# Deformable sampling with 9 x 14 source tiles on 126 partitions instead of 8 x 16 on 128

## The chip, the cores and the metric

The kernel runs on one core of a Trainium2 chip. The metric is the device time of one execution in microseconds (us), given as the median of several runs. One profiled execution supplies the trace from which all durations, waits and transfer rates below are read.

## The reference, cut to what matters

Two layers run on an input of 2 images x 256 channels x 128 x 128 pixels. The first has three branches with dilations 1, 9 and 12. Each branch computes 18 offsets per pixel with a 3x3 convolution, samples the normalised image at nine displaced positions with bilinear weights, and sums the nine samples with one weight per channel and tap.

```python
def _deform_dw(x, offset, w, pad, dil):
    ...
    py = yy[None, None] - pad + ky[None, :, None, None] * dil + off[:, :, 0]
    px = xx[None, None] - pad + kx[None, :, None, None] * dil + off[:, :, 1]
    sampled = _bilinear(x, py, px)
    wk = w.reshape(C, K)
    return jnp.einsum('bckhw,ck->bchw', sampled, wk)
def _branch(x, w_off, w_def, lw, lb, pad, dil):
    off = _conv(x, w_off, pad, dil)
    y = _deform_dw(x, off, w_def, pad, dil)
    return jax.nn.gelu(_ln2d(y, lw, lb), approximate=False)
x1 = _branch(x, off_w1, def_w1, bw1, bb1, 1, 1)
x2 = _branch(x, off_w2, def_w2, bw2, bb2, 9, 9)
x3 = _branch(x, off_w3, def_w3, bw3, bb3, 12, 12)
c = jnp.einsum('bchw,oc->bohw', x, conv_w[:, :, 0, 0]) + conv_b[None, :, None, None]
out = _ln2d(x1 + x2 + x3 + c, n1_w, n1_b)
h = out.transpose(0, 2, 3, 1)
h = jax.nn.gelu(h @ mlp_w1.T + mlp_b1, approximate=False) @ mlp_w2.T + mlp_b2
...
x = x + _L0_conv_ref(_gn(x), ...)
x = x + _L1_conv_ref(_gn(x), ...)      # a 3x3 convolution with ternary weights
```

## The kernel before, in words

The kernel has three stages. In the trace they lie at 0 to about 950 us, 958 to about 6460 us, and from there to the end.

**The first stage** (`phase_a`, once per image, with the group norm's statistics ahead of it) walks over the image four rows at a time. It loads four rows of x (`xa`, issued by ScalarE), normalises them, writes them with pixels in rows and channels in columns to a table in DRAM (`table`, padded with zeros on all sides), and multiplies by the offset weights (`pz`, kept in `zr`). Every eight rows `offsets` adds the shifted parts. `make_hats` (four rows per call) turns each offset into "hats": for each tap, and for each of TR row and TC column distances inside a source tile, the value min(|distance|, 1) - 1. The product of a row hat and a column hat is the bilinear weight of one source pixel. The hats of one four-row group are built on NH = TR + TC rows for each of nine (branch, row tap) pairs, four pairs in one tile `hb` and five in the next, and stored in DRAM as `hats[q, hat, y, kx, x]` (line 432, issued by SP, three `hb` buffers). The DMA's outermost dimension is pairs times hats: 4 x 24 = 96 and 5 x 24 = 120 partitions.

**The second stage** (`sample_near`) does the sampling by matmul. A unit is (image, row step Rt, branch). A source tile is TR x TC pixels of the table by 256 channels, one pixel per partition (line 770): 8 x 16 = 128 pixels serve RI x CI = 2 x 10 output positions with a reach of 3 pixels each way. A row step has NT = 14 tiles, shared by its three branches. For each of the up to three row taps ky of a unit, `load_hats` fetches a row hat `hy` and a column hat `hx`, both for all 128 pixels, two rows, three column taps and 128 columns (line 796; one row hat is read again for all TC pixels, one column hat for all TR). `build` multiplies them into the weight tile `A` (line 816, VectorE; two `A` alternate between units). In `sample`, for each channel half c, each tile is a matmul of 128 pixels x 128 channels by A's 9 taps x 2 rows x 10 columns = 180 (line 889); an f32 matmul appears as two instructions. Two tiles share a PSUM tile `pm` (four of them), which ScalarE copies to `ev` (line 898, three buffers). `accumulate` then adds the nine taps, each times its channel weight, into a ring of image rows for the branch: the first by ScalarE (line 860), the other eight by VectorE (line 867). When a ring has four finished rows, a chain of the class `Tail` is started: layer norm, gelu, the sum of the branches in DRAM (`g12d`), and for the last branch the 1x1 convolution, norm and MLP (lines 573 to 745). The tail's steps are interleaved with the sampling by `tail.advance()`, called at fixed points of `sample`, and ahead of need when a ring row is still to be read.

The order of all compute instructions of this stage is fixed by `pin` (program order on each engine). The loads are on SP's queue, which runs in order. `prepare(u + 2)` is called after the second half's matmuls of unit u: it builds all products of unit u + 2 one after the other and then issues the hat loads of unit u + 3, whose buffers (three `hy`, three `hx`) come free with these products. The source tiles have 20 buffers for 14 in use.

**The third stage** (`phase_c_signs`) is the ternary convolution. It is not touched.

The constants that the change sets anew are these:

```python
RI, CI = 2, 10
TR, TC = RI + 2 * REACH, CI + 2 * REACH
NT = -(-(W + 2 * REACH) // CI)
NH = TR + TC
RINGS = (8, 24, 32)
```

Of the kernel before, what the change touches and what calls it, by code (L numbers as in the profile page):

```python
# [9 lines left out]
F32 = mybir.dt.float32  # L10
I32 = mybir.dt.int32
U32 = mybir.dt.uint32
BF16 = mybir.dt.bfloat16
# [28 lines left out]
RI, CI = 2, 10  # L42
# [3 lines left out]
AO = 12  # L46
WA = 28 + W
NH = TR + TC
HALF = 64
RINGS = (8, 24, 32)  # L50
# [6 lines left out]
XCLS = (0, 1, 2, 8, 9)  # L57
# [10 lines left out]
def conv_preact_kernel(ctx: ExitStack, tc: tile.TileContext, t: dict, out: bass.AP):  # L68
# [5 lines left out]
    NR = (H + 2 * REACH) // RI  # L74
# [202 lines left out]
    def phase_a(b, pool, psum, k, beside):  # L277
# [123 lines left out]
        def make_hats(g, parts, r0):  # L401
# [7 lines left out]
            pl = k["planes"][g % 2]  # L409
# [40 lines left out]
    with ExitStack() as actx:  # L450
        psum = actx.enter_context(tc.tile_pool(name="ps_a", bufs=1, space=PSUM))

        def gps():
# [12 lines left out]
            "planes": [ap.tile([P, 2, NG], BF16, name=f"planes{i}") for i in range(2)],  # L466
# [6 lines left out]
        for b in range(NB):  # L473
# [12 lines left out]
            if b == 0:  # L486
# [6 lines left out]
                pattern = ap.tile([P, NG], F32, name="pattern", tag="xt", bufs=3)  # L493
                nc.sync.dma_start(pattern[HALF : HALF + NPAT], t["pattern"])
                for pl in k["planes"]:
                    nc.vector.tensor_copy(
                        pl[HALF : HALF + NPAT, 1, :], pattern[HALF : HALF + NPAT]
                    )
# [23 lines left out]
    def free(ins):  # L522
        return ins

    class Tail:
# [50 lines left out]
        def normalised(self, z, src, what=None):  # L576
# [10 lines left out]
            for h in range(NB4 // 2):  # L587
                tp = self.bank("tp")
                for j in range(2):
                    for c in range(KC):  # L590
                        i = j * KC + c
                        px = slice((2 * h + j) * P, (2 * h + j + 1) * P)
                        pin(nc.tensor.transpose(tp[:, i * P : (i + 1) * P], src[:, c, px], ident))  # L593
# [78 lines left out]
        def finish(self, b, g, S, other, xn):  # L672
# [16 lines left out]
            yield from self.normalised(z, S)  # L689
# [42 lines left out]
            yield from self.normalised(z, S)  # L732
# [19 lines left out]
    def sample_near(pool, psum, k):  # L752
# [7 lines left out]
        def load_tiles(b, Rt):  # L760

            xts[b, Rt] = []
            for T in range(NT):
                xt = pool.tile([P, C], F32, name="xs", tag="xs", bufs=20)
# [5 lines left out]
                nc.sync.dma_start(xt, src)  # L770
# [11 lines left out]
        def load_hats(u):  # L782
            b, Rt, br = units[u]
            for ky in taps(u):
                i0, i1 = valid(Rt, br, ky)
                hq = hats[b][br * 3 + ky + 1]
                y0 = Rt * RI - REACH - ky * DILS[br] + i0
                hy = pool.tile([P, RI, 3, W], F32, name="hy", tag="hy", bufs=3)
                hx = pool.tile([P, RI, 3, W], F32, name="hx", tag="hx", bufs=3)
                pitch = HY * 3 * W  # L790
                for h, first, dims in (
                    (hy, 0, [[0, TC], [pitch, TR]]),
                    (hx, TR, [[pitch, TC], [0, TR]]),
                ):
                    src = hq[first, y0]
                    nc.sync.dma_start(
                        h[:, i0:i1].rearrange("p i t w -> p (i t w)"),
# [520 lines left out]
```

## Time and profile before

| what | value |
|---|---|
| median of three runs | 7621.91 us (7618.33 to 7638.79) |
| the profiled execution | 7634.92 us, its span 7633.1 us |
| mean granted TensorE clock | 0.97 |
| sampling matmuls, line 889 | 22,288 instructions, 318 ns each as recorded |
| hat loads, line 796 | 2 x 1130 |
| source tile loads, line 770 | 1876 of 128 KB |
| hat stores, line 432 | 64 of 720 KB, 64 of 576 KB |

The execution from which the profile was taken is 13 us above the median. Its time is 1.8 us more than the span, which runs from the first to the last instruction. The recorded duration of a matmul includes the time in which it overlaps its neighbours: a burst of 28 sampling matmuls takes 4.43 us, 158 ns each. Windows of the trace list, for each stretch, its length, the busy time and number of instructions of TensorE, of its weight loads, of VectorE, ScalarE and GpSimd, the granted clock, the mean busy share of the 16 DMA engines, and the GB/s they moved. A DMA share a little above 1 means that packets of one engine overlap.

### The profile page before, as it was taken

Reading aid. Unit: us, or ns where it says so; the run is one execution under the profiler, and the core shown is the slowest. Engines: PE = TensorE matmul, PEld = TensorE weight load, DVE = VectorE, ACT = ScalarE, POOL = GpSimd, SP = SyncE. Lnnn points to the kernel's source line nnn. Section 1 sums busy time; section 2 is a strip of 40 time slices with the busy share of each in tenths; the row PEclk is TensorE's granted clock in tenths of the full one; section 3 lists DMA queues with packets and bytes.
Section 4 is the critical chain, followed back from the end, with each engine's and each line's share of the span. In section 5 each row is a group of like instructions: output and inputs, shape, how many; then the busy total and the mean of one; then the engine's idle time right before and its main releaser. Section 6 shows DMA issues by size and latency. Waiting matters only on the chain. (4 is left out here: it accounts for less than half of the span.)

```text
span 7633.1 us, 114421 instructions
## 1 busy us (share of the span) xinstructions
PE 7040.9 (92%) x37984; PEld 5353.3 (70%) x37984; DVE 6109.5 (80%) x12723; ACT 4832.0 (63%) x10150; POOL 712.8 (9%) x1292
## 2 busy tenths in 40 slices
PE   6899888999999999999988999999999999899999
PEld 3555487777887788887777877887888777444444
DVE  7756557888888888988578888888888986677675
ACT  2344366777777777777676777777777777433232
POOL 0000000111111111111100111111111111000000
PEclk9999989999999999999999999999999999899999
DMA  8866689999999999998699999999999995222121
GB/s 285 265 193 197 181 231 250 248 253 256 256 255 252 254 259 255 258 256 231 180 239 246 254 255 253 256 254 253 251 259 254 254 252 161 90 75 76 69 78 47
DMA packets 856311, 1658.87 MB, mean 217 GB/s; under 512 B 116704, under 2 KB 403216, under 8 KB 851480
## 3 DMA queue, kind: packets, MB, share of 16 engines
q1 hardware_dynamic: 838296, 1617.84, 78.1%
q10 hardware_dynamic: 17408, 33.56, 1.3%
q8 instruction: 304, 4.98, 0.3%
q14 instruction: 303, 2.48, 0.1%
HBM read 1381.02 MB, written 270.06 MB: 216 GB/s over the span
## 5 line engine op out<-in xcount | busy, mean ns | idle before, releaser
L889 PE MATMUL pm<-A,xs 128*128 128x180 f32 (+2 forms) x22288 | 3624.6, 318 | 355.6 <-ACT ev L898 248.8
L889 PEld LDWEIGHTS pm<-A,xs 128*128 128x128 f32 x22288 | 3400.5, 195 | 598.0 <-ACT ev L898 347.0
L867 DVE SCALAR_TENSOR_TENSOR ring<-ev,defw,ring 128x256 f32<-128x256 f32 (+3 forms) x6344 | 2780.4, 459 | 339.1 <-ACT ev L898 159.0
L898 ACT COPY ev<-pm 128x360 f32<-128x360 f32 (+2 forms) x5572 | 2244.9, 449 | 791.3 <-PE pm L889 483.3
L816 DVE TENSOR_TENSOR A<-hy,hx 128x768 f32<-128x768 f32 x1130 | 1026.1, 947 | 413.1 <-DMA hx<-hats 300.6
L1172 PE MATMUL pc<-cring,signs 128*128 128x512 bf16 x4608 | 1005.3, 381 | 20.0 <-ACT cring L1119 13.3
L1172 PEld LDWEIGHTS <-signs 128*128 128x128 bf16 x4608 | 452.0, 98 | 572.8 <-issue 27.0
L614 ACT ACTIVATE T<-T,rs 128x256 f32<-128x256 f32 x1280 | 661.9, 589 | 180.5 <-POOL rs L610 180.4
L607 POOL TENSOR_SCALAR rs<-mv 128x4 f32<-128x4 f32 x320 | 122.8, 384 | 4904.3 <-DVE mv L605 2681.5
L573 PE MATMUL hp<-T,w 128*128 128x512 f32 x1024 | 503.8, 617 | 12.9 <-ACT T L692 12.9
L603 DVE BATCH_NORM_STATS2 st<-T 128x6 f32<-128x256 f32 x1280 | 447.0, 412 | 25.3 <-ACT T L595 25.2
L320 PE MATMUL pz<-wz,xa 128*128 128x486 f32 x1024 | 463.7, 582 | 3.1 <-DVE zr L327 3.1
L573 PE MATMUL h<-hT,w 128*128 128x512 f32 x1024 | 460.1, 592 | 0.0
L642 ACT ACTIVATE T<-zc,bb,bw 128x512 f32<-128x512 f32 x384 | 277.5, 773 | 228.0 <-PE zc L626 227.9
L860 ACT ACTIVATE ring<-ev,defw 128x256 f32<-128x256 f32 (+1 forms) x788 | 392.2, 503 | 24.1
L1180 ACT ACTIVATE o<-xl,l1b 128x1024 f32<-128x1024 f32 x64 | 73.5, 1148 | 501.8 <-DMA out_x<-o 394.8
L626 PEld LDWEIGHTS zc<-ident,T 128*128 128x128 f32 x2560 | 315.0, 147 | 96.3 <-issue 61.9
L626 PE MATMUL zc<-ident,T 128*128 128x128 f32 x2560 | 358.7, 284 | 19.7 <-ACT T L614 13.8
L595 ACT COPY T<-tp 128x512 f32<-128x512 f32 x640 | 340.5, 583 | 42.5 <-PE tp L593 42.3
L609 POOL TENSOR_TENSOR rs<-rs,mhalf 128x4 f32<-128x4 f32 x320 | 365.0, 1141 | 0.0
L1119 ACT CAST cring<-D 128x2048 bf16<-128x2048 f32 (+1 forms) x140 | 245.0, 1755 | 183.4 <-PE pc L1172 125.1
L573 PEld LDWEIGHTS h<-hT,w 128*128 128x128 f32 x1024 | 189.1, 190 | 186.6 <-issue 186.1
(118 smaller groups left out, 5226.4 us busy)
## 6 DMA issues: line engine op xcount, KB each, us to landing
hy<-hats SPq DMA_DIRECT2D x1114, 384.0 KB
hx<-hats SPq DMA_DIRECT2D x1114, 384.0 KB
xs<-table SPq DMA_DIRECT2D x1876, 128.0 KB
g12d<-T SPq DMA_DIRECT2D x128, 512.0 KB
other<-g12d SPq DMA_DIRECT2D x128, 512.0 KB
hats<-hb SPq DMA_DIRECT2D x64, 720.0 KB
hats<-hb SPq DMA_DIRECT2D x64, 576.0 KB
xl<-x1d SPq DMA_DIRECT2D x56, 640.0 KB
```

The lines of the kernel that those rows point to most:

```text
L320: nc.tensor.matmul(pz[:, 0:NZ], lhsT=xt[:, c, r, :], rhs=k["wz"][:, c, :], start=c == 0, stop=c == KC - 1,)
L573: nc.tensor.matmul(out, lhsT=w, rhs=v, start=i == 0, stop=i == n - 1)
L603: pin(nc.vector.bn_stats(st[:, j, :], Tv[:, j, :]))
L609: nc.gpsimd.tensor_tensor(rs[:, 0, :], rs[:, 0, :], mhalf[:, 0:NB4], ALU.pow)
L614: nc.scalar.activation(Tv[:, j, :], Tv[:, j, :], AF.Identity, scale=rs[:, 0, j : j + 1], bias=rs[:, 1, j : j + 1],)
L626: nc.tensor.transpose(zc[:, j * P : (j + 1) * P], Tv[:, j, c * P : (c + 1) * P], ident)
L816: nc.vector.tensor_tensor(dst, hy[:, i0:i1].rearrange("p i t w -> p t i w"), hx[:, i0:i1].rearrange("p i t w -> p t i w"), ALU.mult,)
L860: pin(nc.scalar.mul(dst, src, w))
L867: pin(nc.vector.scalar_tensor_tensor(dst, src, w, dst, ALU.mult, ALU.add))
L889: nc.tensor.matmul(pm[:, j, 0:n], lhsT=xts[b, Rt][T + j][:, c * P : (c + 1) * P], rhs=A[:, m0:m1, AO + (T + j) * CI : AO + (T + j + 1) * C ...
L898: nc.scalar.copy(ev[:, m0:m1, T * CI : (T + 2) * CI].rearrange("p m (t j) -> p t m j", j=CI), pm[:, :, 0:n].rearrange("p t (m j) -> p t m ...
L1172: nc.tensor.matmul(pc[:, bank, :], lhsT=w[:, m * P : (m + 1) * P], rhs=xc[:, i, k, t * JC : (t + 1) * JC, kx : kx + W], start=j == 0, stop ...
```

## The change

The source tile becomes 9 x 14 = 126 pixels for 3 x 8 positions: RI, CI = 3, 8. There are then 17 tiles in a row step and 45 row steps instead of 67. NH becomes 9 + 14 = 23. The matmuls have up to 9 x 3 x 8 = 216 columns. The tiles, hats and products are addressed on 126 partitions (TP).

The weight tile `A` is laid out with WP = 136 columns a row and no gap between rows; columns of one tap that no sum reads may hold values of the neighbouring row. `columns` gives, for each tile, which column taps are read at all; others are left out of the matmul and of the copy. The first tile has a PSUM tile of its own, the other sixteen go in pairs.

The products of a unit are no longer built together: `steps` lists all of them in order, and `build(until)` does the next one, if it belongs to a unit not later than `until`. It is called after the matmuls of each half and, in the first half, also in the middle of the sums. Hats are loaded one transfer at a time (`load_hat`), up to two products ahead, into four buffers with one tag. The rings have 9, 25 and 31 rows, and are read row by row by the tail (`by_row`, `rows`), since a group of four may wrap. `ev` has two buffers, the source tiles 23. The tail is advanced three times in each half instead of twice. Where the row pattern of the hats has a period of 3, three `planes` with their own patterns are used in turn. The scratch space reserved for dynamic DMAs is set to 4096 bytes.

```diff
@@ -39,22 +39,29 @@
 
 REACH = 3
 LIMIT = float(REACH)
-RI, CI = 2, 10
+RI, CI = 3, 8
 TR, TC = RI + 2 * REACH, CI + 2 * REACH
 NT = -(-(W + 2 * REACH) // CI)
 WT = NT * CI + 2 * REACH
-AO = 12
-WA = 28 + W
+TP = TR * TC
+WP = NT * CI
+AO = 16
+KA = 9 * WP + AO
+WA = AO + 3 * KA
 NH = TR + TC
 HALF = 64
-RINGS = (8, 24, 32)
+RINGS = (9, 25, 31)
 BRS = (0, 1, 2)
 NORMS = 3
 VBUFS = 9
 PEAK = 3
 GAP = 2
 LAG = 5
-XCLS = (0, 1, 2, 8, 9)
+XBUFS = NT + 6
+HBUFS = 4
+EBUFS = 2
+TICKS = (5, 11)
+XCLS = (0, 1, 4, 7)
 NPAT = RI + len(XCLS) + 1
 
 
...
-    NR = (H + 2 * REACH) // RI
+    NR = -(-(H + 2 * REACH) // RI)
...
-            pl = k["planes"][g % 2]
+            pl = k["planes"][g % RI]
...
-                xt = pool.tile([P, C], F32, name="xs", tag="xs", bufs=20)
+                xt = pool.tile([P, C], F32, name="xs", tag="xs", bufs=XBUFS)
                 src = bass.AP(
                     table[b].tensor,
                     table[b].offset + (Rt * RI * WT + T * CI) * C,
                     [[C, TC], [WT * C, TR], [1, C]],
                 )
-                nc.sync.dma_start(xt, src)
+                nc.sync.dma_start(xt[0:TP], src)
...
-        def load_hats(u):
+        def columns(br, T):
+
+            dil = DILS[br]
+            t = [
+                i
+                for i, s in enumerate((-dil, 0, dil))
+                if max(0, REACH + s) < (T + 1) * CI
+                and T * CI < min(W + 2 * REACH, W + REACH + s)
+            ]
+            return t[0] * RI, (t[-1] + 1) * RI
+
+        steps = [(u, ky) for u in range(len(units)) for ky in taps(u)]
+        loads = [(u, ky, x) for u, ky in steps for x in range(2)]
+        at = {"load": 0, "build": 0}
+
+        def load_hat(u, ky, x):
+
             b, Rt, br = units[u]
-            for ky in taps(u):
-                i0, i1 = valid(Rt, br, ky)
-                hq = hats[b][br * 3 + ky + 1]
-                y0 = Rt * RI - REACH - ky * DILS[br] + i0
-                hy = pool.tile([P, RI, 3, W], F32, name="hy", tag="hy", bufs=3)
-                hx = pool.tile([P, RI, 3, W], F32, name="hx", tag="hx", bufs=3)
-                pitch = HY * 3 * W
-                for h, first, dims in (
-                    (hy, 0, [[0, TC], [pitch, TR]]),
-                    (hx, TR, [[pitch, TC], [0, TR]]),
-                ):
-                    src = hq[first, y0]
-                    nc.sync.dma_start(
-                        h[:, i0:i1].rearrange("p i t w -> p (i t w)"),
-                        bass.AP(src.tensor, src.offset, dims + [[1, (i1 - i0) * 3 * W]]),
-                    )
-                hbs[u, ky] = hy, hx
-
-        def build(u, ky):
-
+            i0, i1 = valid(Rt, br, ky)
+            hq = hats[b][br * 3 + ky + 1]
+            pitch = HY * 3 * W
+            dims = [[pitch, TC], [0, TR]] if x else [[0, TC], [pitch, TR]]
+            src = hq[x * TR, Rt * RI - REACH - ky * DILS[br] + i0]
+            h = pool.tile([P, RI, 3, W], F32, name="h", tag="h", bufs=HBUFS)
+            nc.sync.dma_start(
+                h[0:TP, i0:i1].rearrange("p i t w -> p (i t w)"),
+                bass.AP(src.tensor, src.offset, dims + [[1, (i1 - i0) * 3 * W]]),
+            )
+            hbs[u, ky, x] = h
+
+        def load_hats():
+
+            while at["load"] < min(len(loads), 2 * at["build"] + HBUFS):
+                load_hat(*loads[at["load"]])
+                at["load"] += 1
+
+        def build(until):
+
+            if at["build"] == len(steps) or steps[at["build"]][0] > until:
+                return False
+            u, ky = steps[at["build"]]
             b, Rt, br = units[u]
             dil = DILS[br]
             i0, i1 = valid(Rt, br, ky)
-            hy, hx = hbs.pop((u, ky))
-
...
+            A = k["A"][u % len(k["A"])]
             dst = bass.AP(
-                Af.tensor,
-                Af.offset + ((ky + 1) * 3 * RI + i0) * WA + AO + REACH - dil,
-                [list(Af.ap[0]), [RI * WA + dil, 3], [WA, i1 - i0], [1, W]],
+                A.tensor,
+                A.offset + AO + (ky + 1) * KA + i0 * WP + REACH - dil,
+                [[A.ap[0][0], TP], [RI * WP + dil, 3], [WP, i1 - i0], [1, W]],
             )
             pin(
                 nc.vector.tensor_tensor(
                     dst,
-                    hy[:, i0:i1].rearrange("p i t w -> p t i w"),
-                    hx[:, i0:i1].rearrange("p i t w -> p t i w"),
+                    hy[0:TP, i0:i1].rearrange("p i t w -> p t i w"),
+                    hx[0:TP, i0:i1].rearrange("p i t w -> p t i w"),
                     ALU.mult,
                 )
             )
+            at["build"] += 1
+            load_hats()
+            return True
 
...
-            for ky in reversed(kys):
-                for dst, src, w in sums[ky]:
-                    pin(nc.vector.scalar_tensor_tensor(dst, src, w, dst, ALU.mult, ALU.add))
+            todo = [s for ky in reversed(kys) for s in sums[ky]]
+            for n, (dst, src, w) in enumerate(todo):
+                if c == 0 and n == len(todo) // 2:
+                    build(u + 1)
+                pin(nc.vector.scalar_tensor_tensor(dst, src, w, dst, ALU.mult, ALU.add))
 
         def sample(u, c):
 
             b, Rt, br = units[u]
             kys = taps(u)
+            if c == 0:
+                while build(u):
+                    pass
             tail.advance()
             if not kys:
                 tail.advance()
-                if c == KC - 1:
-                    prepare(u + 2)
+                tail.advance()
+                build(u + 1 + c)
                 return
-            A = k["A"][u % len(k["A"])].rearrange("p t i w -> p (t i) w")
-            m0, m1 = (kys[0] + 1) * 3 * RI, (kys[-1] + 2) * 3 * RI
-            n = (m1 - m0) * CI
-            ev = pool.tile([P, 9 * RI, NT * CI], F32, name="ev", tag="ev", bufs=3)
-            for T in range(0, NT, 2):
-                if T // 2 == NT // 4:
+            A = k["A"][u % len(k["A"])]
+            y0, y1 = kys[0] + 1, kys[-1] + 2
+            ev = pool.tile([P, 9 * RI, WP], F32, name="ev", tag="ev", bufs=EBUFS)
+            evv = ev.rearrange("p (y m) w -> p y m w", y=3)
+            for T in (0, *range(1, NT, 2)):
+                if T in TICKS:
                     tail.advance()
+                ts = range(T, min(T + 2, NT)) if T else range(1)
+                reach = [columns(br, t) for t in ts]
+                m0, m1 = min(r[0] for r in reach), max(r[1] for r in reach)
+                n = (y1 - y0) * (m1 - m0) * CI
                 pm = psum.tile([P, 2, 256], F32, name="pm", tag="pm", bufs=4)
-                for j in range(2):
+                for j, t in enumerate(ts):
+                    a0 = A.offset + AO + y0 * KA + m0 * WP + t * CI
                     pin(
                         nc.tensor.matmul(
                             pm[:, j, 0:n],
-                            lhsT=xts[b, Rt][T + j][:, c * P : (c + 1) * P],
-                            rhs=A[:, m0:m1, AO + (T + j) * CI : AO + (T + j + 1) * CI],
+                            lhsT=xts[b, Rt][t][0:TP, c * P : (c + 1) * P],
+                            rhs=bass.AP(
+                                A.tensor, a0,
+                                [[A.ap[0][0], TP], [KA, y1 - y0], [WP, m1 - m0], [1, CI]],
+                            ),
                             start=True,
                             stop=True,
                         )
                     )
-                pin(
-                    nc.scalar.copy(
-                        ev[:, m0:m1, T * CI : (T + 2) * CI].rearrange(
-                            "p m (t j) -> p t m j", j=CI
-                        ),
-                        pm[:, :, 0:n].rearrange("p t (m j) -> p t m j", j=CI),
-                    )
-                )
-            if c == KC - 1:
-                prepare(u + 2)
+                src = pm[:, 0 : len(ts), 0:n]
+                if m1 - m0 == 3 * RI:
+                    dst = ev[:, y0 * 3 * RI : y1 * 3 * RI, T * CI : (T + len(ts)) * CI]
+                    dst = dst.rearrange("p m (t j) -> p t m j", j=CI)
+                    src = src.rearrange("p t (m j) -> p t m j", j=CI)
+                else:
+                    dst = evv[:, y0:y1, m0:m1, T * CI : (T + len(ts)) * CI]
+                    dst = dst.rearrange("p y m (t j) -> p t y m j", j=CI)
+                    src = src.rearrange("p t (y m j) -> p t y m j", y=y1 - y0, j=CI)
+                pin(nc.scalar.copy(dst, src))
+            build(u + 1 + c)
             accumulate(u, c, ev, kys)
 
-        def prepare(u):
-
-            if u < len(units):
-                for ky in taps(u):
-                    build(u, ky)
-                if u + 1 < len(units):
-                    load_hats(u + 1)
-
...
-                "A": [pool.tile([P, 9, RI, WA], F32, name=f"A{i}") for i in range(2)],
+                "A": [pool.tile([P, WA], F32, name=f"A{i}") for i in range(2)],
...
 
-    nc = bacc.Bacc("TRN2", target_bir_lowering=False, num_devices=1)
+    nc = bacc.Bacc(
+        "TRN2", target_bir_lowering=False, num_devices=1, dynamic_dma_scratch_size=4096
+    )
```

## The prediction

> **What bounds the kernel now.** I read the page first (busy shares, queues), then the windows by stage, then short windows in which only one kind of transfer is in flight, then the groups and the waits. From the page:
>
> ```profile
> PE 7040.9 (92%) x37984; PEld 5353.3 (70%) x37984; DVE 6109.5 (80%) x12723; ACT 4832.0 (63%) x10150; POOL 712.8 (9%) x1292
> ...
> DMA packets 856311, 1658.87 MB, mean 217 GB/s; under 512 B 116704, under 2 KB 403216, under 8 KB 851480
> ## 3 DMA queue, kind: packets, MB, share of 16 engines
> q1 hardware_dynamic: 838296, 1617.84, 78.1%
> ```
>
> TensorE looks like the bound. The windows of the sampling stage (start, image 0, the change of image, image 1, end) say that it isn't alone; the last two columns are DMA share and GB/s:
>
> ```profile
> 958.00:1300.00 342.00, 285.20 (x1804) 274.76 (x1804) 237.33 (x494) 218.65 (x547) 11.67 (x24) 0.88 0.91 239
> 1300.00:3560.00 2260.00, 2139.00 (x12210) 1813.72 (x12211) 2009.03 (x4531) 1724.15 (x3802) 303.23 (x533) 0.99 0.96 254
> 3560.00:3760.00 200.00, 186.25 (x1122) 151.33 (x1121) 124.67 (x312) 140.26 (x348) 31.89 (x68) 0.91 0.69 195
> 3760.00:6260.00 2500.00, 2340.82 (x13394) 1998.06 (x13391) 2173.73 (x4867) 1877.99 (x4160) 311.54 (x552) 0.98 0.95 250
> 6260.00:6460.00 200.00, 185.66 (x1132) 150.53 (x1132) 147.10 (x362) 142.59 (x344) 34.17 (x68) 0.94 0.67 185
> ```
>
> Over these 5502 us TensorE is busy 5137 (93%) and the DMA engines 311 + 2170 + 138 + 2375 + 134 = 5128 us (93%; 95 to 96% in the two long windows). Both are at their limit, DVE (4692, 85%) and ACT (4104, 75%) are not. What the DMA engines carry decides, so I look at it by kind: only 8 KB rows of x; only hat stores; 2 KB rows; only hat loads (3072 B rows); only source tiles (1 KB rows):
>
> ```profile
> 20.00:30.00 10.00, 0.00 (x0) 0.00 (x0) 8.40 (x15) 0.00 (x0) 0.00 (x0) 1.00 1.00 405
> ...
> 668.00:670.40 2.40, 2.40 (x11) 1.27 (x10) 0.96 (x1) 1.57 (x4) 0.00 (x0) 1.00 0.93 282
> 3010.50:3013.00 2.50, 2.50 (x11) 1.56 (x10) 2.43 (x6) 0.18 (x1) 0.00 (x0) 1.00 1.06 388
> 3035.00:3041.00 6.00, 6.00 (x42) 6.00 (x41) 4.73 (x6) 4.47 (x11) 0.00 (x0) 1.00 1.03 254
> 6140.10:6143.10 3.00, 3.00 (x22) 2.99 (x21) 2.96 (x5) 2.73 (x7) 0.00 (x0) 1.00 1.12 300
> ```
>
> One of 16 engines thus moves 15.9 GB/s of hat loads, 18.8 of source tiles, 24.3 of 2 KB rows, 17.6 of hat stores, 25.3 at best. The stage before, which builds table and hats (image 0, then image 1), has the engines at 83 and 66% and TensorE at 89 and 94%:
>
> ```profile
> 100.00:460.00 360.00, 319.68 (x1365) 184.93 (x1364) 262.47 (x512) 139.43 (x257) 0.38 (x1) 0.97 0.83 254
> 565.00:895.00 330.00, 309.97 (x1361) 179.23 (x1360) 200.05 (x373) 139.14 (x257) 0.00 (x0) 1.00 0.66 192
> ```
>
> The groups that change, and the largest DMA wait of the middle of the stage (total, times, longest):
>
> ```profile
> L889 PE MATMUL pm<-A,xs 128*128 128x180 f32 (+2 forms) x22288 | 3624.6, 318 | 355.6 <-ACT ev L898 248.8
> L889 PEld LDWEIGHTS pm<-A,xs 128*128 128x128 f32 x22288 | 3400.5, 195 | 598.0 <-ACT ev L898 347.0
> L867 DVE SCALAR_TENSOR_TENSOR ring<-ev,defw,ring 128x256 f32<-128x256 f32 (+3 forms) x6344 | 2780.4, 459 | 339.1 <-ACT ev L898 159.0
> L898 ACT COPY ev<-pm 128x360 f32<-128x360 f32 (+2 forms) x5572 | 2244.9, 449 | 791.3 <-PE pm L889 483.3
> L816 DVE TENSOR_TENSOR A<-hy,hx 128x768 f32<-128x768 f32 x1130 | 1026.1, 947 | 413.1 <-DMA hx<-hats 300.6
> ```
> ```profile
> DVE A L816 <- DMA hx<-hats: 180.8, 151, 6.4
> ```
>
> [...] I add, over all issues of the page, rows moved plus one packet for each engine used. With 16 engines wherever the rows allow, 15 for the 64 stores of 120 rows, 9 for the 24 zero fills of 18 rows and 8 for one load of 8 rows this gives 838,296, which is the page's q1 to the packet; with 16 everywhere it would be 240 more. [...]
>
> **The change part by part.** Counts follow from the loops of code and diff.
>
> *Matmuls.* Before, 796 passes (unit and channel half with any tap) x 14 tiles x 2 instructions = 22,288 with 3.797 M columns. After, 536 x 17 x 2 = 18,224 with 3.607 M (216 columns, 144 where an edge column block is left out). At 180 columns a burst of 28 takes 4.43 us (158 ns each[...]). [...] so -230 us.
>
> *Evacuation.* 5572 copies become 4824. From 464 ns at 360 columns and 372 at 240 I take 520 at 432: -200 us of ACT, with the first-row products -250. *Accumulation.* 6344 become 4496 (rings of 9, 25 and 31 rows split runs of three rows at their wrap). 480 ns at 256 columns, 346 at 128: 1.05 ns a column, 614 at 384; summed over all widths 2508 against 2912: -385 us of DVE. *Weight products.* 1130 become 756[...]. These three are not the bound now, and become less so. I cost them at nothing; TensorE and DMA hide them.
>
> *Order and buffers.* A pass lasts some 10 us (5502/536), of which DVE works 8. With two ev instead of three, the copies of pass n+2 wait for the sums of pass n: about 2 us of margin. The products in the middle of the sums put four sums behind a wait for hats, and these the copies, and these the matmuls. Hats are loaded two products ahead instead of three, but each covers three rows. Rings have 4, 4 and 4 spare rows instead of 4, 4 and 6, so more tail steps may be drawn forward. SP issues 1512 + 1530 loads instead of 2260 + 1876. I take 0; the ends are -40 (smoother loads) and +100.
>
> *Loads of the sampling stage.* Hats 882 -> 870 MB, tiles 246 -> 197 MB, the tail's 235 MB unchanged. But the slowest dimension becomes 14 (and 126 in SBUF): 14 engines. Time of one busy engine, before: 55.2 MB/15.9 + 15.4/18.8 + 14.7/21.3 (tail loads and stores, a mean of 341 GB/s over a longer stretch) = 3.47 + 0.82 + 0.69 = 4.98 ms. After: 62.2/15.9 + 14.1/18.8 + 14.7/21.3 = 3.91 + 0.75 + 0.69 = 5.35 ms, 7.5% more. On the 5128 us measured: 5510. Of today's 374 us without traffic, 128 are at the change of image and the end and stay; of the other 246 I keep half, since TensorE asks less. 5510 + 128 + 123 = 5761, +260 us (all kept +385, none +139). If memory, not the engine, limits the hats (their rows repeat, and they are slower than 1 KB rows), 14 engines carry the same 254 GB/s; then TensorE decides: -230 to 0. The trace has no load on 14 engines; I take +260.
>
> *Hat stores of the stage before.* NH falls from 24 to 23, so stores of 96 and 120 rows become 92 and 115: 4 engines and 5 instead of 16 and 15, 23 rows of 6144 B = 141 KB each. Eight image rows need four stores, so engines 0 to 3 get 565 KB: 32.1 us at 17.6 GB/s, 22.3 at 25.3. Their other traffic: eight rows take 27.6 us in image 0 and 25.7 in image 1 (from the issue times of the stores), times 0.83 and 0.66, less 9.4 us of stores (166 KB at 17.6): 13.5 and 7.6 us. Sums: 45.6 and 39.7 (slow rate), 35.8 and 29.9 (fast). Against 27.6 and 25.7, 16 groups each: +512 or +198. Three hb buffers cannot absorb that; ACT's |.| waits for a free hb, behind it the evacuations, behind them TensorE. I take 21 GB/s: +350 us.
>
> Sum on the profiled execution (7634.9, span 7633.1): +350 + 260 = 8245; the median of the runs is 13 us lower: 8230.
>
> **The rivals.** A, forecast, engines limit both stages: 7960 to 8520. B, the stores are slow, the sampling loads are not limited by the number of engines: TensorE sets sampling (-230 to 0), 7600 to 8150, about 7850. For it: repeated rows are slower than any others. Against: 192 KB loads with 1536 B rows at the picture's edge ran no slower per byte than 3072 B[...]. C, faster: the rows are spread over more engines[...]. Then the engines need 5128 x 0.955 = 4900 us, TensorE's -230 is kept, less about 20: 7425. It decides from 7 engines for the stores on (2.54 MB over 7 engines at 21 GB/s is 17.3 us, plus 7.6 stays under 25.7), with 16 for the loads. Against it stands the packet count. D, slower still: on top of A two ev and the products inside the sums stall in-order queues that now wait for late hats, up to +100 us and more: above 8520.
>
> **Numbers.** A 0.52, B 0.28, C 0.11, D 0.09. The range 7700 to 8540 leaves out C, D and a little of B. Faster (by over 0.3%, about what this measurement can tell from no change): C and an edge of B, 0.13; same 0.03; slower 0.84.
>
> **What would show it.** q1 should hold 665,824 packets; 673,432 would mean 16 engines everywhere, and C. In the first stage TensorE below 80%, ACT waiting for hats<-hb, and eight rows in about 37 us. In sampling a DMA share near 14/16 = 0.87 as a mean of 16 with hats alone at about 222 GB/s, TensorE at 85 to 88%, DVE's wait for hats above 1000 us. Hats alone at 250 GB/s or more means B. A busy TensorE (95%) and DVE waits as today make the forecast wrong.

## The result and the profile after

The changed kernel takes 8256.62 us as the median of four runs (8243.17 to 8282.95), the kernel before 7620.12 us in the same series (7613.19 to 7638.79). The ratio is 1.0835, with a 95% interval of 1.0802 to 1.0868. The forecast was 8230 us. The profiled execution after took 8257.77 us.

The page of the kernel after, its engines, queue and the groups that changed (matmuls, copies to `ev`, sums, weight products):

```profile
PE 7047.4 (85%) x33920; PEld 5280.9 (64%) x33920; DVE 5718.4 (69%) x10502; ACT 4672.8 (57%) x9218; POOL 717.6 (9%) x1292
...
q1 hardware_dynamic: 665824, 1552.63, 59.3%
...
L933 PE MATMUL pm<-A,xs 126*128 126x216 f32 (+3 forms) x18224 | 3490.8, 347 | 461.1 <-ACT ev L953 234.0
...
L953 ACT COPY ev<-pm 128x432 f32<-128x432 f32 (+6 forms) x4824 | 2124.0, 475 | 1373.2 <-PE pm L933 978.6
L903 DVE SCALAR_TENSOR_TENSOR ring<-ev,defw,ring 128x357 f32<-128x357 f32 (+7 forms) x4496 | 2406.2, 560 | 316.0 <-ACT ev L953 185.5
L847 DVE TENSOR_TENSOR A<-h 126x1152 f32<-126x1152 f32 (+2 forms) x756 | 1013.7, 1341 | 882.9 <-DMA h<-hats 544.6
```

Every engine that computes is busy as long as before, to within 1%, or shorter, fewer bytes move, and the kernel is 8% longer. So time has gone into waits. Where they lie shows in the windows, the first stage (image 0, image 1) and then sampling (start, image 0, change of image, image 1, end); the last two columns are DMA share and GB/s:

```profile
100.00:600.00 500.00, 387.56 (x1491) 220.06 (x1490) 280.04 (x545) 152.63 (x284) 0.38 (x1) 0.88 0.56 191
720.00:1160.00 440.00, 352.76 (x1369) 198.08 (x1367) 199.69 (x372) 136.08 (x254) 0.00 (x0) 0.89 0.41 137
1230.00:1600.00 370.00, 286.01 (x1573) 274.96 (x1574) 224.54 (x370) 208.20 (x495) 14.86 (x24) 0.82 0.71 221
1600.00:3960.00 2360.00, 2064.64 (x10171) 1730.59 (x10172) 1785.64 (x3460) 1615.78 (x3300) 289.10 (x516) 0.94 0.72 225
3960.00:4200.00 240.00, 208.08 (x1233) 172.81 (x1231) 144.61 (x334) 159.71 (x388) 38.86 (x72) 0.93 0.61 191
4200.00:6850.00 2650.00, 2285.40 (x11427) 1925.24 (x11428) 1981.31 (x3806) 1799.79 (x3708) 312.32 (x552) 0.94 0.73 225
6850.00:7080.00 230.00, 200.93 (x1161) 165.46 (x1159) 156.15 (x344) 153.14 (x358) 34.42 (x64) 0.93 0.56 175
```

In the first stage TensorE is at 78 and 80% (89 and 94% before). The first weight product of sampling starts at 1230.1 us instead of 956.9: 273 us lost. The first matmul of the third stage is at 7217.2 us instead of 6595.0, 622 later, so about 349 us are lost in sampling; the third stage is as long as before. In these windows of sampling TensorE is busy 5045 of 5850 us, where it was 5137 of 5502. The busy time fell by 92 us and the time without work rose from 365 to 805.

And the DMA engines are not at their limit either: a share of 0.72 to 0.73 of 16 is 0.83 of 14, the number that the packets of the loads give (experiment 1). With (nearly) only hat loads in flight, the kernel after shows:

```profile
2277.50:2291.00 13.50, 10.98 (x50) 10.32 (x50) 12.09 (x23) 9.13 (x18) 2.16 (x4) 0.75 0.81 258
2958.00:2964.00 6.00, 4.20 (x27) 3.92 (x26) 3.68 (x6) 3.92 (x9) 0.00 (x0) 1.00 0.87 255
5868.00:5874.00 6.00, 6.00 (x25) 4.44 (x25) 5.38 (x14) 3.88 (x8) 1.28 (x3) 1.00 0.89 332
5310.00:5316.00 6.00, 5.90 (x32) 5.35 (x31) 0.39 (x1) 4.65 (x9) 0.00 (x0) 0.79 0.90 220
```

The trace also keeps the size of every packet, and a hat row of the kernel after has 4608 B: in the first stretch 98% of the bytes are hats, in the others all. The rate differs from stretch to stretch. If the whole of sampling is cut into pieces of 6 us, and those are kept in which hats are over 97% of the bytes and the engines in use are busy all the time (a share of at least 0.84 for 14, 0.96 for 16), then the median of 71 pieces after is 260 GB/s, and that of 176 pieces before is 248. Fourteen engines carry 18.6 GB/s each where sixteen carried 15.5. The prediction had named 250 as the sign of its rival B. Rival B's time was wrong as well, though, since neither TensorE nor the engines then set the pace. What does is to be looked for in the waits (total, times, longest), here of all engines after:

```profile
DVE A L847 <- DMA h<-hats: 544.6, 172, 14.0
...
ACT ev L953 <- DVE ring L903: 330.5, 110, 13.6
...
ACT xn L678 <- DMA xn<-in_x: 197.8, 31, 13.8
```

and of TensorE alone, after:

```profile
PE pm L933 <- ACT ev L953: 234.0, 146, 8.5
PE pc L583 <- ACT xn L678: 177.3, 20, 13.1
PE pm L933 <- DVE A L847: 140.9, 49, 33.7
```

Two of these are new. Before, TensorE waited 31.3 us for a weight product and 0.8 us for `xn`, the normalised input that the tail multiplies in its 1x1 convolution:

```profile
PE pm L889 <- ACT ev L898: 248.8, 185, 4.3
...
PE pm L889 <- DVE A L816: 31.3, 9, 6.3
```

One of the new stalls, in the timeline after (start, duration, what ran, in brackets the idle time before it):

```profile
3001.68 1.69 SPq L819 DMA_DIRECT2D h<-hats  x2
...
3003.42 0.54 SPq L674 DMA_DIRECT2D xn<-in_x  x1
...
3014.17 1.33 ACT L678 ACTIVATE xn<-xn,negmean 128x512 f32<-128x512 f32 x2 [12.65 <-DMA xn<-in_x]
...
3014.95 2.92 PE L583 MATMUL pc<-xn,convw 128*128 128x512 f32 x3 [12.04 <-ACT xn L678]
```

The tail's input is issued behind two hat loads of 126 x 4608 B = 581 KB each, and ScalarE starts on it 10.75 us after its issue. Behind ScalarE waits TensorE; the copies to `ev` stand behind the normalisation in ScalarE's order too.

### The profile page after: what moved, and what is told of

Read it like the earlier page. It is cut to its first block, busy times and chain, and to the rows that moved or that the text cites. A ratio compares the mean times of both kernels' runs of the same rounds, so it can differ in the third digit from the quotient of the medians.

```text
span 8255.7 us, 100744 instructions
## 1 busy us (share of the span) xinstructions
PE 7047.4 (85%) x33920; PEld 5280.9 (64%) x33920; DVE 5718.4 (69%) x10502; ACT 4672.8 (57%) x9218; POOL 717.6 (9%) x1292
## 3 DMA queue, kind: packets, MB, share of 16 engines
q1 hardware_dynamic: 665824, 1552.63, 59.3%
## 5 line engine op out<-in xcount | busy, mean ns | idle before, releaser
L933 PE MATMUL pm<-A,xs 126*128 126x216 f32 (+3 forms) x18224 | 3490.8, 347 | 461.1 <-ACT ev L953 234.0
L933 PEld LDWEIGHTS pm<-A,xs 126*128 126x128 f32 x18224 | 3235.0, 200 | 735.5 <-ACT ev L953 318.5
L953 ACT COPY ev<-pm 128x432 f32<-128x432 f32 (+6 forms) x4824 | 2124.0, 475 | 1373.2 <-PE pm L933 978.6
L903 DVE SCALAR_TENSOR_TENSOR ring<-ev,defw,ring 128x357 f32<-128x357 f32 (+7 forms) x4496 | 2406.2, 560 | 316.0 <-ACT ev L953 185.5
L847 DVE TENSOR_TENSOR A<-h 126x1152 f32<-126x1152 f32 (+2 forms) x756 | 1013.7, 1341 | 882.9 <-DMA h<-hats 544.6
L327 PE MATMUL pz<-wz,xa 128*128 128x486 f32 x1024 | 522.7, 645 | 11.0 <-DVE zr L334 10.9
L583 PE MATMUL pc<-xn,convw 128*128 128x512 f32 x512 | 274.8, 687 | 177.3 <-ACT xn L678 177.3
L434 ACT ACTIVATE hb<-ph 92x512 f32<-92x512 f32 (+1 forms) x384 | 213.1, 595 | 340.4 <-PE ph L427 172.7
L718 ACT ACTIVATE hT<-hp,b 128x512 f32<-128x512 f32 x256 | 176.5, 689 | 323.0 <-PE hp L583 323.0
L583 PEld LDWEIGHTS hp<-T,w 128*128 128x128 f32 x1024 | 195.7, 198 | 245.1 <-issue 224.4
```

What stands on the lines that cost most here:

```text
L327: nc.tensor.matmul(pz[:, 0:NZ], lhsT=xt[:, c, r, :], rhs=k["wz"][:, c, :], start=c == 0, stop=c == KC - 1,)
L583: nc.tensor.matmul(out, lhsT=w, rhs=v, start=i == 0, stop=i == n - 1)
L847: nc.vector.tensor_tensor(dst, hy[0:TP, i0:i1].rearrange("p i t w -> p t i w"), hx[0:TP, i0:i1].rearrange("p i t w -> p t i w"), ALU.mult,)
L903: pin(nc.vector.scalar_tensor_tensor(dst, src, w, dst, ALU.mult, ALU.add))
L933: nc.tensor.matmul(pm[:, j, 0:n], lhsT=xts[b, Rt][t][0:TP, c * P : (c + 1) * P], rhs=bass.AP(A.tensor, a0, [[A.ap[0][0], TP], [KA, y1 - y0 ...
L953: pin(nc.scalar.copy(dst, src))
```

## Experiments: which part costs what

Ratios are to the kernel before, run in the same series, with 95% intervals. Differences in us are between medians; the kernel before had 7620 to 7634 us in the four series.

**1. The stores of the first stage.** One row that nothing reads is added to the hats, so that 4 x 24 = 96 and 5 x 24 = 120 rows are stored again, as before. All else is as in the change.

```diff
-NH = TR + TC
+NH = TR + TC + 1
...
-    hats = dram("hats", [NOFF // 6, TR + TC, HY, 3, W])
+    hats = dram("hats", [NOFF // 6, NH, HY, 3, W])
```

> The changed kernel with hats built and stored on 24 rows instead of 23 (the 24th is never read), so that the stores have 96 and 120 rows again; the loads keep 14 engines. Both theories: the first stage ends at about 951 us as before the change instead of 1226, the total falls by about 275 us to about 7980 us, and the sampling stage keeps its length of about 5850 us.

Measured: 7987.2 us, 1.0475 (1.0458 to 1.0493), 269 us less than the change, and the third stage begins at 6944.0 us, 273 earlier. The windows of its first stage are those of the kernel before again (0.83 and 0.66 there, against 0.56 and 0.41 after):

```profile
100.00:460.00 360.00, 321.29 (x1384) 185.12 (x1383) 263.38 (x515) 142.92 (x264) 0.38 (x1) 0.98 0.85 255
565.00:895.00 330.00, 304.24 (x1331) 175.98 (x1330) 195.81 (x365) 133.47 (x246) 0.00 (x0) 0.99 0.66 187
```

So 23 hat rows instead of 24 make the loss in the first stage, by how the stores divide and not by their size: this kernel stores more. How they divide shows in the number of packets. Besides the rows moved, the traces hold packets of 4 B, 81,376 before and 56,432 after on q1. They are read here as one for each engine that takes part; that is an inference, since no view names an engine. In sampling (1230 to 7080 us) the kernel after has 49,202 of them; 14 for each load of 126 rows (380,880 rows) and 16 for each transfer of 256 rows of the tail (110,080 rows) make 49,200. In this experiment:

```profile
q1 hardware_dynamic: 667808, 1556.20, 62.4%
```

That is 1984 more than after. The 128 stores have 576 rows more, and the other 1408 are what 16 engines instead of 4 for 64 stores, and 15 instead of 5 for the other 64, add up to. The following experiments on the large tile start from this version.

**2. The number of engines of the sampling loads.** On top of experiment 1, tiles and hats are loaded in a pattern of 8 x 16 pixels, whose slowest dimension is 16 and which fills 128 partitions.

```diff
-                    [[C, TC], [WT * C, TR], [1, C]],
+                    [[C, 16], [WT * C, 8], [1, C]],
...
-            dims = [[pitch, TC], [0, TR]] if x else [[0, TC], [pitch, TR]]
+            dims = [[pitch, 16], [0, 8]] if x else [[0, 16], [pitch, 8]]
```

> As e1_rows24, and each source tile and each hat is loaded for an 8 x 16 pattern of pixels on all 128 partitions (16 engines) instead of 9 x 14 on 126, so the values sampled are others; matmuls, products, buffers and order stay. Theory E (14 engines limit sampling): it falls by 200 to 350 us to about 7700 us. Theory Q (the engines' number matters little, since 14 of them carried about 250 GB/s of hats as 16 did before; the shallow buffers and the order on SP's queue cost the time): it falls by less than 80 us, to 7900 us or more.

Measured: 7965.6 us, 1.0442 (1.0423 to 1.0460). The number of packets, 679,976, rises by what 16 engines instead of 14 and two rows more for each of the 3042 loads give (12,168), but only 22 us are gained, of the 260 that the forecast put on this. The same stretch of sampling in experiment 1 (14 engines), then in this one (16 engines):

```profile
1300.00:3700.00 2400.00, 2096.56 (x10383) 1758.25 (x10382) 1815.67 (x3527) 1646.73 (x3362) 289.71 (x529) 0.94 0.72 225
```

```profile
1300.00:3700.00 2400.00, 2083.99 (x10396) 1748.46 (x10395) 1825.14 (x3536) 1646.07 (x3370) 297.42 (x528) 0.94 0.92 229
```

The DMA share goes from 0.72 to 0.92 while the matmuls in the stretch stay within 0.2% and the GB/s within 2%. It rises because each packet takes longer: a hat row of 4608 B is recorded with 235 ns on average in experiment 1 and with 311 here. A share near 1 was read as "at the limit" in the prediction; here the same traffic shows either share. With hats alone (98% of the bytes in the stretch below) the 16 engines move 229 GB/s, 14.3 each. The median of 181 pieces of 6 us, taken as above, is 235, not more than the 14 engines had:

```profile
3012.00:3020.00 8.00, 1.69 (x11) 1.48 (x9) 5.31 (x10) 0.30 (x1) 0.32 (x2) 0.80 1.02 229
```

**3. One engine's own rate.** Does an engine have a limit of its own for hats? In the kernel before, each hat load is split into two transfers of 64 partitions, whose slowest dimension is 8. This was timed once.

```diff
+                    for half in range(2):
...
+                                src.tensor, src.offset + 8 * half * dims[0][0],
+                                [[dims[0][0], 8], dims[1], [1, (i1 - i0) * 3 * W]],
```

> The kernel before with each hat load split into two DMAs of 64 partitions, whose slowest dimension of 8 puts each on 8 engines. If the engine limits hats (15.9 GB/s each), hats alone move 127 GB/s and the kernel takes 10.5 ms or more. If memory limits them, 8 engines at the 25.3 GB/s seen at best reach about 200 GB/s, and the kernel stays below 9 ms.

Measured: 10631.6 us, with hats alone:

```profile
3000.00:3005.00 5.00, 0.00 (x0) 0.00 (x0) 4.82 (x19) 0.00 (x0) 2.07 (x4) 0.50 0.51 130
3039.00:3045.00 6.00, 6.00 (x43) 5.80 (x42) 3.38 (x11) 5.69 (x13) 2.29 (x4) 1.00 0.52 129
3890.00:3896.00 6.00, 6.00 (x30) 4.45 (x30) 5.79 (x19) 4.26 (x9) 0.30 (x1) 0.92 0.52 208
```

The shares of 0.51 and 0.52 are those of 8 engines of 16. In the first two stretches these carry 16.2 GB/s each, about half the bytes; in the third they carry 26 each. The median of 258 pieces of 6 us is 144 GB/s, against 248 with 16 engines, and the kernel takes 3 ms more. So what the forecast expected of fewer engines exists at 8: the hats are slower, and TensorE is busy 2247 of the 3500 us from 1500 to 5000, where it was 2139 of 2260 in the long window before. But 15.9 GB/s is not what one engine can do at most, and from 14 engines to 16 nothing is gained. What else holds the rate of the hats was not tried.

**4. The lead of the third product.** The change spreads the three products of unit u + 1: one after the second half's matmuls of unit u - 1, one after the first half's of unit u, and the last in the middle of the sums of that first half, close to the matmuls that need it. The edit moves the product inside the sums half a unit earlier.

```diff
-                if c == 0 and n == len(todo) // 2:
-                    build(u + 1)
+                if c == 1 and n == len(todo) // 2:
+                    build(u + 2)
```

> As e1_rows24, with the product in the middle of the sums moved from the first half to the second, so that of the three products of a unit two are made a whole pass or more before its matmuls and the last one before the sums, not in their middle. Theory P (the last product of a unit comes too late for TensorE): 60 to 150 us faster than e1_rows24, about 7880 us. Theory D (two ev and hats two products ahead): within 30 us of e1_rows24, since a product earlier only waits longer for its hats.

Measured: 7883.6 us, 1.0322 (1.0292 to 1.0353), 104 us less than experiment 1. TensorE's wait for a product falls from 112.4 to 70.6 us. Its wait for `xn` falls too, from 185.2 to 91.8, presumably since the move also changes when the hats are asked for, and so what stands ahead of the tail's loads on SP. The 104 us are therefore not shown to be the product's lead alone. Two other waits rise (experiment 1, then this one):

```profile
DVE A L847 <- DMA h<-hats: 605.7, 191, 14.3
...
PE pm L933 <- ACT ev L953: 219.4, 143, 6.0
```

```profile
DVE A L847 <- DMA h<-hats: 766.4, 231, 19.5
...
PE pm L933 <- ACT ev L953: 397.7, 189, 9.9
```

This fits hats that are asked for earlier and come no earlier: VectorE waits in front of its sums instead, and through the sums and the `ev` buffers the wait reaches TensorE again.

**5. The tail's loads on a queue of their own.** On top of experiment 1, `other`, `xn` and `xr` are issued by ScalarE instead of SP.

```diff
-            nc.sync.dma_start(xn, x[b].rearrange("(k p) h w -> p k (h w)", p=P)[:, :, cols])
+            nc.scalar.dma_start(xn, x[b].rearrange("(k p) h w -> p k (h w)", p=P)[:, :, cols])
```

> As e1_rows24, with the tail's three loads (other, xn, xr) issued by ScalarE instead of SP, so that they don't stand behind the hats in the same queue. Theory T (ScalarE waits 181 us for xn, and TensorE behind it 160 us, because a load of the tail lands some 10 us after its issue): 100 to 160 us faster than e1_rows24, about 7860 us. Theory D (depth of ev and hats sets the pace, the tail's waits are taken from the same slack): less than 50 us, 7940 us or more.

Measured: 7874.4 us, 1.0322 (1.0297 to 1.0348), 113 us less than experiment 1. The normalisation's wait for `xn` falls (experiment 1, then this one), and TensorE's behind it from 185.2 to 57.7 us:

```profile
ACT xn L678 <- DMA xn<-in_x: 207.6, 29, 13.6
```

```profile
ACT xn L678 <- DMA xn<-in_x: 96.8, 37, 10.9
```

Whether a load was late because of the bytes queued ahead of it, or because SP stood still ahead of its issue, this doesn't tell apart.

**6. Both together**, experiments 4 and 5 in one kernel.

> e1_rows24 with both e3_tailq and e7_earlier: the 9 x 14 tile with stores on 16 and 15 engines, the tail's loads on ScalarE's queue, and the products earlier. If the two gains of 113 and 104 us are separate: about 7770 us. If they are taken from the same slack (theory D: ev and hats bound it next): 7820 us or more.

Measured: 7800.7 us, 1.0224 (1.0206 to 1.0242): 187 us less than experiment 1, of the 217 that the two gave singly, between the two expectations. TensorE now waits for `ev` most, and 166 us over the kernel before remain:

```profile
PE pm L933 <- ACT ev L953: 468.5, 214, 10.6
PE pm L933 <- DVE A L847: 74.6, 28, 27.1
...
PE pc L583 <- ACT xn L678: 49.9, 20, 6.6
```

**7. The change without its tile.** The code of the change with the tile of before: 2 x 10 positions, 128 partitions, rings, copies and hats as deep as before (three `ev`, hats three products ahead). What stays of the change is mainly the spread products, the new layout of `A`, the edge columns with a tile alone at each end of a row, and hats loaded one by one.

```diff
-RI, CI = 3, 8
+RI, CI = 2, 10
...
-RINGS = (9, 25, 31)
+RINGS = (8, 24, 32)
...
-HBUFS = 4
-EBUFS = 2
-TICKS = (5, 11)
-XCLS = (0, 1, 4, 7)
+HBUFS = 6
+EBUFS = 3
+TICKS = (7,)
+XCLS = (0, 1, 2, 8, 9)
```

> The changed kernel with the old tile: RI, CI = 2, 10, rings of 8, 24 and 32 rows, three ev, six hat buffers, two tail steps a pass; what is left of the change is the products spread over the passes, the edge columns left out and a tile alone at each end. Theory E: stores and loads are on 16 engines again, so about the time of the kernel before or a little less, 7550 to 7640 us. Theory Q: if the spread products and the new order of the loads are what costs, most of the 350 us of the sampling stage stays: 7750 to 7970 us.

Measured: 7719.8 us, 1.0131 (1.0109 to 1.0153), 89 us slower than before with the tile and all depths of before, and between the two expectations. One place in its timeline:

```profile
2036.55 0.95 DVE L847 TENSOR_TENSOR A<-h 128x768 f32<-128x768 f32 x1
...
2037.60 4.70 PE L932 MATMUL pm<-A,xs 128*128 128x180 f32 x18 [6.94 <-issue]
```

TensorE stands still 6.94 us and starts 0.1 us after the end of the product. The list of waits puts such gaps down to "issue" (383.9 us in all), since it finds no releaser; by its time this one is the late third product.

**8. The same with the product moved earlier**, that is experiments 7 and 4 together.

> As e4_oldtile (old tile, 7720 us), with the same move as e7_earlier. Theory P: most of its 90 us over the kernel before goes: 7640 us or less, and the waits of nearly 7 us ahead of a burst of sampling matmuls go. Theory D has nothing to say here (three ev, six hat buffers): no change.

Measured: 7580.5 us, 0.9930 (0.9909 to 0.9950), the fastest of all kernels here, and 139 us faster than experiment 7. With the product earlier, most of the waits under "issue" are gone (experiment 7, then this one), and TensorE's wait for `xn` was small in both (5.3 and 3.8 us), so that here the lead of the product isn't mixed with that:

```profile
PE pm L932 <- issue: 383.9, 63, 7.8
```

```profile
PE pm L932 <- issue: 132.7, 33, 9.6
```

DMA share and rate are now a little higher than before (0.96 and 254):

```profile
1300.00:3560.00 2260.00, 2108.77 (x12315) 1813.85 (x12314) 2009.79 (x4562) 1734.35 (x4155) 314.80 (x540) 0.98 0.98 257
```

**9. All three products together again**, on experiment 7: after the second half's matmuls, as in the kernel before.

```diff
-            build(u + 1 + c)
+            if c == 1:
+                while build(u + 2):
+                    pass
             accumulate(u, c, ev, kys)
```

> As e4_oldtile, with all three products of a unit made together after the second half's matmuls of the unit two before, as in the kernel before; of the change are left the edge columns, the two tiles alone and the single tag of hats. Theory P: about 7620 us, within 30 us of the kernel before, perhaps up to 50 us less for the columns left out. If it stays at 7700 us, the edges' form costs the 90 us and not the place of the products.

Measured: 7648.2 us, 1.0021 (1.0013 to 1.0030). So the rest of the change, edge columns and layout of `A` among it, brings no gain by itself (18 us are lost), and spreading the products brings 68 us if they stay ahead (experiment 8) and costs 72 if the last one is late (experiment 7).

**10. The tail's queue on experiment 8.**

> e8_old_earlier (old tile, earlier products, 7581 us) with the tail's loads on ScalarE's queue. Its loads of 393 KB leave less to wait behind; a gain of 0 to 40 us, 7540 to 7580 us, ahead of both kernels.

Measured: 7587.4 us, 0.9944 (0.9927 to 0.9960): no gain over experiment 8, where 0 to 40 us were expected. The queue edit pays on the large tile, not on this one.

**11. Two `ev` instead of three, in the kernel before.**

```diff
-name="ev", tag="ev", bufs=3
+name="ev", tag="ev", bufs=2
```

> The kernel before with two ev instead of three. Theory E: no effect, within 40 us of 7620 us. Theory Q: the second buffer's margin is one of the costs: 100 to 200 us slower, about 7770 us, with ScalarE's copies waiting for VectorE's sums.

Measured: 7691.1 us, 1.0084 (1.0067 to 1.0101), 60 us slower. That lies between the two expectations. ScalarE's wait for a free `ev` rises from 75.3 to 459.5 us.

**12. Both depths of the change on experiment 8:** two `ev`, and hats two products ahead.

```diff
-HBUFS = 6
-EBUFS = 3
+HBUFS = 4
+EBUFS = 2
```

> e8_old_earlier with the buffers of the changed kernel: two ev instead of three and hats two products ahead (four buffers) instead of three (six). Theory D (depth is what the 9 x 14 tile still lacks): 100 to 250 us slower, 7680 to 7830 us. If it stays within 40 us of 7581 us, what remains with the large tile is its geometry: longer products and passes.

Measured: 7995.2 us, 1.0479 (1.0459 to 1.0499), 415 us slower than experiment 8 and more than expected. Its waits:

```profile
ACT ev L952 <- DVE ring L903: 722.4, 345, 7.0
DVE A L847 <- DMA h<-hats: 708.0, 371, 10.5
...
PE pm L932 <- ACT ev L952: 564.7, 401, 6.1
```

Products spread among the sums are affordable with three `ev` and hats well ahead (102.0 us of waiting for hats in experiment 8), and not with both depths cut; which of the two costs more was not tried. The size doesn't carry over to the large tile as it is: two products ahead are two image rows each here and three there.

## Why the total was right, and which step of it was not

The total came out within 27 us, but by luck: the forecast's mechanism holds for only one of its two terms.

**Hat stores: right, the size too large.** The packet count, 665,824, is the number worked out, to the packet, with stores on 4 and 5 engines and loads on 14. TensorE fell to 78 and 80%, and ScalarE waits for the stores of `hb` (after, then before):

```profile
ACT hb L434 <- DMA hats<-hb: 158.8, 36, 6.8
```

```profile
ACT hb L427 <- DMA hats<-hb: 11.7, 9, 3.0
```

Eight rows take 35.7 us in image 1 (ten groups from 727.25 to 1084.36 us) where about 37 were named. The term was +350 us and measured 269 (experiment 1). "I take 21 GB/s" was too slow a rate of one engine. A stretch of stores, after (by packet sizes three quarters of its bytes are stores, the rest loads of x):

```profile
836.00:840.00 4.00, 2.50 (x5) 1.26 (x5) 0.00 (x0) 2.56 (x5) 0.00 (x0) 0.70 0.30 116
```

A share of 0.30 is 4.8 engines of 16, with 116 GB/s: 24.2 GB/s each, near the fast end (25.3) of the two rates that the prediction had. The 17.6 at its slow end came from a stretch in which 16 engines stored at once. The rate alone doesn't account for the 269, though: with 24.2 the prediction's own sum gives 9.2 and 5.2 us for eight rows, about +230 in all. By the issue times of the stores, from the first to the last of an image, image 0 grew by 113 us and image 1 by 118, where the sum at 21 has 205 and 141; the rest of the 273 us lies between and behind the images. So image 0 is what was too large, where the prediction added most other traffic to the stores; why it costs less there was not tried.

**Sampling loads: the step that failed.** "62.2/15.9" took the rate of one of sixteen engines, 15.9 GB/s, as what an engine can do. It was a sixteenth of what the hats get in all: fourteen engines move 260 GB/s (median). Of the +260 us of this term some 22 are there (experiment 2), in a kernel whose other waits were still in place. The named signs failed with it: a share near 0.87 (0.72), 222 GB/s (260), a wait for hats above 1000 us (544.6). The sign that held, TensorE at 85 to 88% (86%), doesn't tell the two causes apart.

**Order and buffers: "I take 0", ends -40 and +100.** This is where sampling's loss is. The two moves that could be made on the large tile give back 187 us (third product earlier 104, the tail's loads off SP's queue 113, less the overlap, since both shorten the wait for `xn`). Neither was in the list as a price: the products inside the sums were seen as a delay of the sums, not as a product that comes late for its own matmuls; and the tail's loads were counted in bytes, not in what stands ahead of them in the queue. Some 166 us of the sampling loss stay open. Two `ev` and hats two products ahead are the likely rest: part of each wait that is removed returns as a wait for `ev` (468.5 us in experiment 6), and on the small tile two `ev` cost 60 us in the kernel before (experiment 11) and both depths 415 where the products are spread (experiment 12). On the large tile with a third `ev` it wasn't tried, and neither were 16 engines on top of experiment 6: with the other waits gone, they could be worth more than 22 us.

**TensorE.** 18,224 matmuls as counted; -230 us, an estimate of the author's for which no view gives the ground, became -134 (3624.6 to 3490.8). The granted clock in the long windows is 0.94 instead of 0.98 to 0.99. If the matmuls' time goes with the clock, which no run here tests by itself, then 3490.8 scaled by 0.94/0.985 is 3331, an estimate from these figures and below the 3395 that -230 us leaves, so that the clock would be enough for the difference. Why it fell wasn't tried. It is lower in each kernel of the large tile and rises as their stalls go (mean 0.927 after, 0.938 in experiment 1, 0.953 in experiment 6, 0.970 before).

**The rest.** Sums -374 us of VectorE (-385 predicted), products -12 (priced at nothing; 1351 ns each at 1152 columns and 952 at 768, and 756 of them instead of 1130), copies -121 of ScalarE (-200). No run prices these savings by themselves. That they are worth nothing is not shown: the waits for `ev` say that the sums do hold up TensorE at times.

**The rivals.** B was right about the loads' rate and wrong to conclude that TensorE then decides. What was held against it, the short rows, is in the trace before: rows of 1536 B take 91 ns on average, 17.0 GB/s, and rows of 3072 B 196 ns, 15.7 GB/s. Still 14 engines carried 260. D named the waits that do decide, as something on top of A; they stand in place of A's second term. C fell with the packet count. Two terms that were wrong, +260 that is nearly nothing and 0 that is some 330, with the stores' 80 us too many, made a sum that is right by luck.

## What to carry to other kernels

Here one row more in a scratch tensor, with stores on 16 and 15 engines instead of 4 and 5 by the packet counts, is worth 269 us. So when a tile size is changed, count the packets of every transfer, the small stores too, and compare them with the rows moved. When work is spread to smooth a queue, keep its lead over its consumer: on the small tile the same three products were worth -68 or +72 us by half a unit of lead. The DMA share didn't tell here whether the engines were the bound: it was 0.72 on 14 engines and 0.92 on 16, in kernels 22 us apart. Change the number of engines, or look for the rate of one kind of transfer alone at two counts, before a time is worked out from it.

## What the runs showed of the hardware that was not expected

- Hats, whose rows are read repeatedly, move at a median of 144 GB/s on 8 engines (nine tenths of the pieces of 6 us between 127 and 205), 260 on 14 (225 to 328), and on 16 at 248 with rows of 3072 B (235 to 272) and 235 with rows of 4608 B (223 to 250).
- The same traffic shows a DMA share of 0.72 on 14 engines and 0.92 on 16, and one of its rows takes 235 and 311 ns.
- The issue of a source tile load of 126 rows, on 14 engines, takes SP 786 ns (median), that of one of 128 rows, on 16, 548 ns. Minimum, median and maximum of the kernel after:

```profile
L783 SPq DMA_DIRECT2D xs<-table x1530: 781/786/1546, 1211.5 to 7033.7; - x192
```

The 548 ns are the median of the kernel before and of experiments 2 and 8.
